# A two-layer transformer kernel: layernorms, expert work, shift rows and weight loads placed anew in its first attention layer

## The chip, the cores and the metric

The kernel runs on one core of a Trainium2 chip. The metric is the device time of one execution in microseconds; the kernel before takes 1212.92 us (median of three runs, 1212.03 to 1213.0). All arithmetic is float32, apart from a mask and a bias fold that go through TensorE in bfloat16 pieces.

## What is computed

Four sequences of 512 tokens with 256 features pass through four residual steps, each on a layernormed input:

```
x = x + attention_0(layernorm(x))   # 16 heads of 16, causal, over the 512 tokens of a sequence
x = x + experts_0(layernorm(x))     # for each output feature: router over 8 experts, the top 2 of the softmax
x = x + attention_1(layernorm(x))   # 16 query heads of 128, 4 key/value heads, over the batch of 4 at each position
x = x + mlp_1(layernorm(x))         # gated, 2048 wide, 4-bit weights with scales
```

In the experts a token gets 256 x 8 router logits, so each of the 256 output features picks its own two experts; the result is the weighted sum of those two experts' outputs. Router and experts have biases.

## The kernel before

**Tiling.** `xres` holds all 2048 tokens on chip, as 16 tiles of 128 tokens. Block j (0 to 3) is tiles 4j to 4j+3: tokens 128j to 128j+127 of all four sequences. Causal attention of block j needs the keys of blocks 0 to j.

**Attention 0.** `norm_pieces` normalises a block (statistics and scaling on VectorE, the inverse root on GpSimd, called POOL in the profile). `prepare` (L561) transposes the result on TensorE, `project` (L524) makes queries and keys, two heads' groups at a time, and sends them by 8 DMAs each into the tile `qk`, and `values` (L546) makes the values in `va`. In `qk` each head has 32 partitions: row 0 is a shift row, rows 1 to 16 hold the head's features. The shift row of the keys is 1 and that of the queries minus the row's greatest score, so that the second scores come out shifted. `blank` (L455) prepares `qk` and `va` of a later block with memsets on POOL.

The work is cut into 44 batches (L594): block 0 has 4 (one for each sequence, all 16 heads), block 1 has 8 (8 heads each), blocks 2 and 3 have 16 each (4 heads each). In batch n's turn of the loop at L776, the program emits `greatest(n+1)` (scores, L606), `shift(n)` (L639: the maxima of batch n are transposed, one 128x128 transpose for each group of four heads, and subtracted), `mask(n+1)` (L621: causal mask added by matmuls, then maxima by VectorE), a slot of filler, `mixed(n-1)` (L691: probabilities times values), `powers(n)` (L654: second scores, exponentials on ScalarE, a causal select on POOL), and a second slot of filler. `divided` (L712) finishes a sequence: transpose, division, transpose back, and after the last sequence of a block the output product and the residual.

**The planner.** TensorE, VectorE and POOL execute in program order here. What fills the slots comes from generators in the list `streams`: each yields `need(engine, cost, gap, cond)` ahead of a piece, and `fill` (L140) runs through the list from the front and takes pieces while the engine's budget for this slot is above zero, the gap in slots since that stream's last piece has passed, and the condition holds. Budgets for TensorE are 4.0 and 4.0 in block 0, 2.0 and 2.4 in block 1, and less after; VectorE gets 2.6. The streams are the next block's `prepare`, `divided`, `fold_pieces` (L234: biases added to the weights of router and experts by a matmul and two additions), `hidden_pieces` (L256: layernorm and transposes of a finished block for the experts), `logit_pieces` (router products), `weight_pieces` (top 2 and softmax weights on VectorE and ScalarE), `result_pieces` (expert products) and `addition_pieces`. Products of router and experts that are not done within attention 0 are spread over attention 1 by the counter `products_left` (L254, L1082).

**Shared things.** Small matmul results go to a pool `dn` of two PSUM buffers; scores to a pool of five. SP issues most DMAs: x, the projections' outputs, and the router and expert weights `rw` and `ew` (`load_pair`, L515), 16 transfers of 256 KB, two after each of batches 0 to 7. The biases come as 96 rows (three copies) to `bs`, and POOL splits them into bfloat16 parts in `blanks` (L488).

**Start.** Three idle matmuls run when `w_project` has landed; then all of `prepare(0)`, `greatest(0)` and `mask(0)` precede the loop.

Of the kernel before, what the change touches and what calls it, by code (L numbers as in the profile page):

```python
# [32 lines left out]
def tile_transformer(  # L33
# [200 lines left out]
    def fold_pieces():  # L234
# [3 lines left out]
        for i, w in enumerate((rw, ew)):  # L238
            for c in range(4):
                yield need(  # L240
                    "DVE", 1.4, cond=lambda i=i, c=c: slot >= loaded.get((i, c), slot) + 3
# [189 lines left out]

    with ExitStack() as l0:
# [12 lines left out]
        shift_row = mask32[:, 0:1]  # L445


        qk = w0.tile([P, 4, NBLK + 2, NS, P], F32, name="qk")
        maxes = [w0.tile([P, 4, 4, 32], F32, name=f"mx{i}") for i in range(2)]
# [5 lines left out]
        def blank(j, i):  # L455

            keys = qk[:, :, j].rearrange("p g s q -> p g (s q)")
            if i == 4:
                to = va.shape[1] if j == NBLK - 1 else (j + 1) * per_block
                nc.gpsimd.memset(va[:, j * per_block : to], 1.0)  # L460
                nc.gpsimd.memset(keys[96:97], 1.0)
            elif i:
                nc.gpsimd.memset(keys[32 * i - 32 : 32 * i - 31], 1.0)
            else:
                nc.gpsimd.memset(keys, 0.0)
# [4 lines left out]
            shift_row.unsqueeze(1).to_broadcast([P, 4, 512]),  # L470
# [11 lines left out]
        bs = a3.tile([P, 2, 512], F32, tag="pt", name="bs")  # L482
        nc.sync.dma_start(out=bs[0:96], in_=bias)
# [4 lines left out]
        def blanks(xn):  # L488
# [6 lines left out]
            for i in range(5):  # L495
                blank(1, i)
# [3 lines left out]
            br = a3.tile([P, 512], F32, tag="pt", name="br")[0:96]  # L500
            bh = a1.tile([P, 512], BF16, tag="oq", name="bh")[0:96]
# [22 lines left out]
        def project(j, xT, half, stage, i):  # L524
# [9 lines left out]
            if i:  # L534
                to = 4 + j % 2
                for r in range(8):
# [3 lines left out]
                        out=qk[h + 1 : h + 17, 2 * half + r // 4, j : to + 1 : to - j].rearrange(  # L540
# [20 lines left out]
        def prepare(j):  # L561

            out = []
            yield from norm_pieces(j, b1, b2, out)
            if not j:
                blanks(out[0])
            xT = a1.tile([P, 2, NS, P], F32, tag="xT0", name=f"xT0_{j}")
            for hc in range(2):
                yield need("PE", 0.5, 1 - hc)
                ps = transposed(out[0], hc, ps_dn, "dn", f"x0_ps{j}_{hc}")  # L570
                nc.scalar.copy(
# [5 lines left out]
            normed.clear()  # L577
            for half in range(2):
                if j or half:
                    stage = a1.tile([P, 2, 512], F32, tag="stage", name=f"stage{j}_{half}")  # L580
                else:
                    stage = b2.tile([P, NE, HID], F32, tag="lg", name="stage0")
                    stage = stage.rearrange("p e o -> p (e o)")[:, :1024].rearrange(
                        "p (i q) -> p i q", i=2
                    )
                for i in range(2):
                    yield need("PE", 1.75, 0 if half or i else 1)
                    project(j, xT, half, stage, i)
                if half == (not j):
                    for s in (0, 2):  # L590
                        yield need("PE", 1.75)
                        values(j, xT, s)

# [27 lines left out]
        def mask(n):  # L621
# [4 lines left out]
            for ps in tiles:  # L626
                for b in range(nb):
                    to = b * nk + j * P
                    nc.tensor.matmul(  # L629
                        ps[:, to : to + P], lhsT=ident_h, rhs=later,  # L630
                        start=False, stop=b == nb - 1,
                    )
            for h, ps in enumerate(tiles):
                nc.vector.tensor_reduce(  # L634
                    maxes[n % 2][:, :nb, h, 0],
# [3 lines left out]
        def shift(n):  # L639
# [3 lines left out]
            ps = ps_mm.tile([P, 4, P], F32, tag="mm", name=f"mxT_{n}")  # L643
            for b in range(len(gs)):
                nc.tensor.transpose(  # L645
                    ps[:, b], maxes[n % 2][:, b].rearrange("p h d -> p (h d)"), ident
                )
            g, nb = gs[0], len(gs)
            q = qk[:, g : g + nb, 4 + j % 2, s, :]
            nc.vector.tensor_tensor(q, q, ps[:, :nb], ALU.subtract)  # L650
# [61 lines left out]
        def divided(j, s):  # L712
# [27 lines left out]
            for t in (0, 2):  # L740
                yield need("PE", 1.75, 1)
# [10 lines left out]
                yield need("DVE", 0.7, 1)  # L752
# [3 lines left out]
            streams.insert(fold_at, Stream(hidden_pieces(j)))  # L756
# [9 lines left out]
        for piece in prepare(0):  # L766
            pass
        nc.sync.dma_start(out=wo, in_=w_out.rearrange("(k p) o -> p k o", p=P))
        greatest(0)
        mask(0)  # L770
        fold = Stream(fold_pieces())
        streams += [
            fold, Stream(addition_pieces()), Stream(counted(weight_pieces())), Stream(result_pieces()),
            Stream(logit_pieces()),
        ]
        for n in range(NBT):  # L776
            j, s, gs = batches[n]
            if (not n or batches[n - 1][0] != j) and j + 1 < NBLK:
                inputs = Stream(prepare(j + 1))
                streams.insert(0, inputs)  # L780
            if n + 1 < NBT and batches[n + 1][0] != j:
                while inputs.next is not None:
# [8 lines left out]
            fill(PE=(4.0, 2.0, 1.8, 1.6)[j], DVE=2.6)  # L791
            with tc.high_priority(offset=AHEAD):
                if n:
                    mixed(n - 1)
                powers(n)
            if n and batches[n - 1][2][-1] == 3:
                streams.insert(0, Stream(divided(*batches[n - 1][:2])))
            fill(PE=(4.0, 2.4, 2.2, 2.0)[j], DVE=2.6)
            if n < 8:
                w, dram = (rw, router_w) if n < 4 else (ew, expert_w)  # L800
                load_pair(w, dram, 2 * n % 8)
                load_pair(w, dram, 2 * n % 8 + 1)
                loaded[n // 4, n % 4] = slot
            if 1 <= n < 11:
                blank(2 + (n - 1) // 5, (n - 1) % 5)
            if n in (2, 6):
                load_x(n // 4 + 2)
# [447 lines left out]
```

## Time and profile before

| | |
|---|---|
| median of the runs | 1212.92 us |
| profiled execution | 1213.42 us |
| its span in the profile | 1211.7 us |
| mean granted TensorE clock | 0.989 |
| attention 0, experts beside it | to about 420 us |
| attention 1, rest of the experts beside it | about 420 to 880 us |
| MLP | about 880 us to the end |

The profile is of one execution on the chip. Engines are PE (TensorE's matmuls), PEld (its weight loads, which overlap matmuls), DVE (VectorE), ACT (ScalarE), POOL (GpSimd) and SP (which only issues DMAs; SPq and ACTq lines are issues). A group or a line in order of time gives the source line, the engine, the operation, output and inputs by their tile names, and the count; in brackets stands idle time of that engine just before, and what ended it. A float32 matmul counts as two instructions. The clock is the share of full TensorE speed that was granted.

### The profile page before, as it was taken

The numbers are of one execution on the slowest core, as the hardware profiler recorded it, in microseconds if no ns is written. First come the engines' busy times: TensorE is split into PE (matmuls) and PEld (weight loads), VectorE is DVE, ScalarE is ACT, GpSimd is POOL, SyncE is SP. The second block draws the span as 40 slices with busy tenths as digits, with TensorE's granted clock in tenths as the row PEclk, the third lists the DMA queues.
The fourth block names the chain that finished last, engine by engine and source line by source line (L and its number), as shares of the span: only waits on it lengthen the run. The fifth ranks groups of instructions, "written<-read, shape, count | busy, mean of one in ns | idle before, by whom it ended". The sixth has DMA issues, their size and how long they took to land.

```text
span 1211.7 us, 18780 instructions
## 1 busy us (share of the span) xinstructions
PE 1168.9 (96%) x7278; PEld 679.8 (56%) x7278; DVE 802.6 (66%) x1780; ACT 485.5 (40%) x1101; POOL 121.1 (10%) x155
## 2 busy tenths in 40 slices
PE   6979999999999898999999999999999999999998
PEld 3656555555555543555555555656645456475487
DVE  2555589898887848737886395798499853735710
ACT  1233455664555444434444345355344321312300
POOL 8333321121111000000000000000000000000000
PEclk9899999999999998999999999999999999999999
DMA  7122102000000040000000001021020000000000
GB/s 221 17 56 54 19 4 34 2 1 1 2 1 2 27 147 1 1 1 1 1 1 1 1 1 36 10 55 43 1 62 9 1 1 17 1 1 18 0 1 35
DMA packets 21305, 26.78 MB, mean 22 GB/s; under 512 B 5120, under 2 KB 14592, under 8 KB 21216
## 3 DMA queue, kind: packets, MB, share of 16 engines
q1 hardware_dynamic: 20544, 24.40, 7.6%
q10 hardware_dynamic: 672, 1.18, 0.4%
q8 instruction: 57, 0.93, 0.3%
q14 instruction: 32, 0.26, 0.1%
HBM read 19.27 MB, written 2.10 MB: 18 GB/s over the span
## 4 chain that ended last, share of the span: by engine, by line
PE 81%; DVE 12%; ACT 2%; DMA 2%; issue 1%; SPq 1%; POOL 0%; ACTq 0%; DVEq 0%; POOLq 0%
PE qk_ps L928 10%; PE o L1019 9%; PE y L1175 9%; PE g L856 8%; PE u L856 8%; PE eo L226 8%; PE lg_ps L226 7%; PE s L614 4%; DVE mx L634 3%; PE s L664 3%; PE av L700 2%; PE v_ps L910 2%; PE qk_ps L529 2%; PE s L941 1%; PE a L999 1%
## 5 line engine op out<-in xcount | busy, mean ns | idle before, releaser
L928 PE MATMUL qk_ps<-xT,wqkv 128*128 128x512 f32 x320 | 148.7, 599 | 0.6 <-ACT qT L932 0.6
L226 PE MATMUL lg_ps<-rw,xT 128*128 128x512 f32 x256 | 123.8, 607 | 3.7 <-ACT xT L895 1.7
L226 PE MATMUL eo<-ew,xT 128*128 128x512 f32 x256 | 122.0, 600 | 1.3 <-ACT part L315 1.0
L1019 PE MATMUL o<-wpj,oT 128*128 128x256 f32 x512 | 119.8, 382 | 0.0
L634 DVE TENSOR_REDUCE mx<-s 128x1 f32<-128x384 f32 (+3 forms) x176 | 100.5, 634 | 20.3 <-PE s L629 20.3
L1175 PE MATMUL y<-wd,it 128*128 128x256 f32 x512 | 111.8, 379 | 0.0
L1019 PEld LDWEIGHTS o<-wpj,oT 128*128 128x128 f32 x512 | 95.9, 190 | 28.1 <-issue 15.1
L1175 PEld LDWEIGHTS y<-wd,it 128*128 128x128 f32 x512 | 97.1, 190 | 14.9 <-issue 2.2
L928 PEld LDWEIGHTS qk_ps<-xT,wqkv 128*128 128x128 f32 x320 | 59.3, 190 | 70.0 <-issue 60.2
L673 ACT ACTIVATE pt<-s 128x512 f32<-128x512 f32 (+1 forms) x176 | 83.7, 561 | 34.4 <-PE s L664 34.3
L856 PE MATMUL g<-xT,wgu 128*128 128x512 f32 x192 | 90.4, 593 | 0.0
L856 PE MATMUL u<-xT,wgu 128*128 128x512 f32 x192 | 90.2, 592 | 0.0
L315 ACT ACTIVATE part<-eo,c 128x256 f32<-128x256 f32 x128 | 53.7, 473 | 81.5 <-PE eo L226 76.9
L683 POOL TENSOR_SCALAR_AFFINE_SELECT pt<-pt 128x256 f32<-128x256 f32 (+2 forms) x88 | 55.2, 632 | 268.6 <-ACT pt L673 268.1
L1153 ACT ACTIVATE th<-sq 128x512 f32<-128x512 f32 x64 | 40.3, 629 | 87.6 <-DVE sq L1152 87.6
L177 POOL TENSOR_TENSOR ln_rs<-rs_v,minus_half 128x4 f32<-128x4 f32 x16 | 18.0, 1127 | 563.3 <-DVE rs_v L176 457.9
L226 PEld LDWEIGHTS lg_ps<-rw,xT 128*128 128x128 f32 x256 | 46.5, 192 | 49.0 <-issue 36.9
L226 PEld LDWEIGHTS eo<-ew,xT 128*128 128x128 f32 x256 | 46.4, 190 | 45.8 <-issue 37.0
L614 PE MATMUL s<-qk 32*128 32x128 f32 (+3 forms) x512 | 69.7, 478 | 1.3 <-DMA qk<-stage 0.5
L214 DVE TENSOR_TENSOR xres<-xres,y 128x256 f32<-128x256 f32 x16 | 6.7, 421 | 92.2 <-PE y L1175 92.2
L650 DVE TENSOR_TENSOR qk<-qk,mxT 128x128 f32<-128x128 f32 (+2 forms) x44 | 15.2, 346 | 77.0 <-PE mxT L645 69.3
L289 ACT COPY lg<-lg_ps 128x512 f32<-128x512 f32 x64 | 37.6, 587 | 64.5 <-PE lg_ps L226 64.3
(233 smaller groups left out, 1831.2 us busy)
## 6 DMA issues: line engine op xcount, KB each, us to landing
qk<-stage SPq DMA_DIRECT2D x56, 64.0 KB, 2.4
wqkv<-in_w_qkv SPq DMA_DIRECT2D x8, 320.0 KB, 6.0
rw<-in_router_w SPq DMA_DIRECT2D x8, 256.0 KB, 4.8
ew<-in_expert_w SPq DMA_DIRECT2D x8, 256.0 KB, 5.0
wpj<-in_w_proj SPq DMA_DIRECT2D x1, 2048.0 KB, 11.9
out<-xres SPq DMA_DIRECT2D x4, 512.0 KB, 2.6
xres<-in_x SPq DMA_DIRECT2D x3, 512.0 KB, 8.1
dq_wgu<-in_gate_w SPq DMA_DIRECT2D x8, 128.0 KB, 2.4
```

The costliest lines, as they stand in the source:

```text
L226: nc.tensor.matmul(ps, lhsT=xT[:, hc, (g % 4) * P : (g % 4 + 1) * P], rhs=w[:, hc, 2 * pair : 2 * pair + 2, :].rearrange("p e o -> p (e o) ...
L289: nc.scalar.copy(lg[:, 2 * pair : 2 * pair + 2, :].rearrange("p e o -> p (e o)"), ps)
L315: nc.scalar.mul(part[:, e % 4], ps[:, i], c[:, e : e + 1])
L614: nc.tensor.matmul(tiles[h][:, b * nk : (b + 1) * nk].rearrange("p (c k) -> p c k", k=P), lhsT=queries(j, g)[r, s], rhs=qk[r, g, : j + 1, ...
L634: nc.vector.tensor_reduce(maxes[n % 2][:, :nb, h, 0], ps[:, : nb * nk].rearrange("p (b k) -> p b k", b=nb), AX.X, ALU.max,)
L673: nc.scalar.activation(pt[:, i, : nb * nk], tiles[2 * pair + i][:, : nb * nk], AF.Exp, scale=0.25)
L683: nc.gpsimd.affine_select(out=last, in_=last, compare_op=ALU.is_ge, fill=0.0, base=0, pattern=pattern, channel_multiplier=-1,)
L856: nc.tensor.matmul(ps, lhsT=wgu[:, w, half, jj, par * P : (par + 1) * P], rhs=xT[:, half, :], start=half == 0, stop=half == 1,)
L928: nc.tensor.matmul(ps, lhsT=wqkv[:, hc, kv, h, :], rhs=xT[:, hc, :], start=hc == 0, stop=hc == 1,)
L1019: nc.tensor.matmul(ys[t // 2][:, t % 2], lhsT=state["o"][:, h, t * P : (t + 1) * P], rhs=wpj[:, HPK * kv + h, :], start=kv == 0 and h == 0 ...
L1153: nc.scalar.activation(th, sq, AF.Tanh, scale=0.7978845608028654)
L1175: nc.tensor.matmul(ps, lhsT=it[:, c // 2, c % 2, t * P : (t + 1) * P], rhs=wd[:, c // 2, c % 2, :], start=c == 0, stop=c == 2 * NJ - 1,)
```

## The change

- **Four shift rows to a head.** Each head has rows 0 to 3 for shifts and its features in rows 4 to 19. Keys of group i have a 1 in row i alone. All maxima of a batch lie in one 128x128 tile, so `shift` makes one transpose, whose result is subtracted from all groups of the batch; `mask` makes one matmul for each score tile, with the mask repeated along the columns. `blank` writes one group's keys of a block with one copy (512 columns) in place of a memset of all groups and four one-row memsets.
- **Blocks 1 to 3 normalised ahead.** Block 1 is normalised before the loop, right after block 0, and its transposes follow block 0's projections (copied out of PSUM by VectorE); its projections are a stream from the start. `prepare(2)` enters at batch 1 and `prepare(3)` at batch 7, in place of batches 4 and 12; for them values come before queries and keys, and queries and keys wait until the batches that read the old queries are done.
- **Block 0's tokens for the experts at once.** Its two output products come in one slot, and `hidden_pieces(0)` goes to the front of the list.
- **Pieces evenly by slot.** TensorE's budgets in block 0 are 2.0 and 2.4 in place of 4.0 and 4.0; folds come one to a slot.
- **Loads.** Router and expert weights are loaded four transfers after each of batches 0 to 3; x of blocks 2 and 3 after batches 0 and 2 (before: 2 and 6). The biases are loaded three times as 8 rows into a tile cleared by VectorE, and are split on POOL after block 1's blanking.

```diff
-                    "DVE", 1.4, cond=lambda i=i, c=c: slot >= loaded.get((i, c), slot) + 3
+                    "DVE", 1.4, 1, cond=lambda i=i, c=c: slot >= loaded.get((i, c), slot) + 3
...
-        maxes = [w0.tile([P, 4, 4, 32], F32, name=f"mx{i}") for i in range(2)]
+        maxes = [w0.tile([P, 4, 32], F32, name=f"mx{i}") for i in range(2)]
...
             if i == 4:
                 to = va.shape[1] if j == NBLK - 1 else (j + 1) * per_block
                 nc.gpsimd.memset(va[:, j * per_block : to], 1.0)
-                nc.gpsimd.memset(keys[96:97], 1.0)
-            elif i:
-                nc.gpsimd.memset(keys[32 * i - 32 : 32 * i - 31], 1.0)
             else:
-                nc.gpsimd.memset(keys, 0.0)
+                nc.gpsimd.tensor_copy(
+                    qk[:, i, j].rearrange("p s q -> p (s q)"),
+                    mask32[:, i : i + 1].to_broadcast([P, 512]),
+                )
...
-        bs = a3.tile([P, 2, 512], F32, tag="pt", name="bs")
-        nc.sync.dma_start(out=bs[0:96], in_=bias)
+        bs = b1.tile([P, 2, 512], F32, tag="hi4", name="bs")
+        nc.vector.memset(bs, 0.0)
+        for i in range(3):
+            nc.sync.dma_start(out=bs[32 * i : 32 * i + 8], in_=bias)
...
-                        out=qk[h + 1 : h + 17, 2 * half + r // 4, j : to + 1 : to - j].rearrange(
+                        out=qk[h + 4 : h + 20, 2 * half + r // 4, j : to + 1 : to - j].rearrange(
...
+        def projections(j, xT):
+            if j > 1:
+                for s in (0, 2):
+                    yield need("PE", 1.75, 1, cond=lambda: blanked > 5 * j - 10)
+                    values(j, xT, s)
             for half in range(2):
...
+                for i in range(2):
+                    yield need(
+                        "PE", 1.75, 0 if half or i else 1,
+                        cond=lambda: j < 2 or done >= 8 * j - 12 and blanked >= 5 * j - 5,
                     )
                     project(j, xT, half, stage, i)
...
             for ps in tiles:
-                for b in range(nb):
-                    to = b * nk + j * P
-                    nc.tensor.matmul(
-                        ps[:, to : to + P], lhsT=ident_h, rhs=later,
-                        start=False, stop=b == nb - 1,
-                    )
+                nc.tensor.matmul(
+                    ps[:, : nb * nk].rearrange("p (b k) -> p b k", b=nb)[:, :, j * P :],
+                    lhsT=ident_h, rhs=later.unsqueeze(1).to_broadcast([P, nb, P]),
+                    start=False, stop=True,
+                )
...
-            ps = ps_mm.tile([P, 4, P], F32, tag="mm", name=f"mxT_{n}")
-            for b in range(len(gs)):
-                nc.tensor.transpose(
-                    ps[:, b], maxes[n % 2][:, b].rearrange("p h d -> p (h d)"), ident
-                )
+            ps = ps_mm.tile([P, P], F32, tag="mm", name=f"mxT_{n}")
+            nc.tensor.transpose(ps, maxes[n % 2].rearrange("p h g -> p (h g)"), ident)
             g, nb = gs[0], len(gs)
             q = qk[:, g : g + nb, 4 + j % 2, s, :]
-            nc.vector.tensor_tensor(q, q, ps[:, :nb], ALU.subtract)
+            nc.vector.tensor_tensor(
+                q, q, ps.unsqueeze(1).to_broadcast([P, nb, P]), ALU.subtract
+            )
...
-                yield need("PE", 1.75, 1)
+                yield need("PE", 1.75, 1 if j or not t else 0)
...
-                yield need("DVE", 0.7, 1)
+                if j:
+                    yield need("DVE", 0.7, 1)
...
-            streams.insert(fold_at, Stream(hidden_pieces(j)))
+            streams.insert(fold_at if j else 0, Stream(hidden_pieces(j)))
...
-        for piece in prepare(0):
+        nc.sync.dma_start(out=wo, in_=w_out.rearrange("(k p) o -> p k o", p=P))
+        both = [[], []]
+        for j in range(2):
+            for piece in norm_pieces(j, b1, b2, both[j]):
+                pass
+            normed.clear()
+            if not j:
+                blanks(both[0][0])
+                xT = a1.tile([P, 2, NS, P], F32, tag="xT0", name="xT0_0")
+                for piece in inputs_T(0, both[0][0], xT):
+                    pass
+        for i in range(5):
+            blank(1, i)
+        split_biases()
+        for piece in projections(0, xT):
             pass
-        nc.sync.dma_start(out=wo, in_=w_out.rearrange("(k p) o -> p k o", p=P))
+        xT = unused("xT0_1", "p (h s q) -> p h s q", h=2, s=NS)
+        for piece in inputs_T(1, both[1][0], xT):
+            pass
         greatest(0)
         mask(0)
+        inputs = {1: Stream(projections(1, xT))}
+        done = blanked = 0
...
-            if (not n or batches[n - 1][0] != j) and j + 1 < NBLK:
-                inputs = Stream(prepare(j + 1))
-                streams.insert(0, inputs)
+            if n in (1, 7):
+                to = 2 if n == 1 else 3
+                inputs[to] = Stream(prepare(to))
+                streams.insert(0, inputs[to])
...
-            fill(PE=(4.0, 2.0, 1.8, 1.6)[j], DVE=2.6)
+            fill(PE=(2.0, 2.0, 1.8, 1.6)[j], DVE=2.6)
...
-            fill(PE=(4.0, 2.4, 2.2, 2.0)[j], DVE=2.6)
-            if n < 8:
-                w, dram = (rw, router_w) if n < 4 else (ew, expert_w)
-                load_pair(w, dram, 2 * n % 8)
-                load_pair(w, dram, 2 * n % 8 + 1)
-                loaded[n // 4, n % 4] = slot
-            if 1 <= n < 11:
-                blank(2 + (n - 1) // 5, (n - 1) % 5)
-            if n in (2, 6):
-                load_x(n // 4 + 2)
+            fill(PE=(2.4, 2.4, 2.2, 2.0)[j], DVE=2.6)
+            if n < 4:
+                w, dram = (rw, router_w) if n < 2 else (ew, expert_w)
+                for i in range(4):
+                    load_pair(w, dram, 4 * n % 8 + i)
+                    loaded[n // 2, (4 * n % 8 + i) // 2] = slot
+            for _ in range(1 + (n < 2) if blanked < 10 else 0):
+                blank(2 + blanked // 5, (blanked + 4) % 5)
+                blanked += 1
+            if n in (0, 2):
+                load_x(n // 2 + 2)
```

## The prediction

> **What bounds the kernel now.** I read the page's first part, then busy time in stretches of the span, then TensorE's instructions in order of time, then the groups, then the queue that issues transfers.
>
> ```profile
> span 1211.7 us, 18780 instructions
> PE 1168.9 (96%) x7278; PEld 679.8 (56%) x7278; DVE 802.6 (66%) x1780; ACT 485.5 (40%) x1101; POOL 121.1 (10%) x155
> ```
>
> TensorE (PE) is the bound: 1168.9 of 1211.7 us, so a change can win only by filling its 42.8 idle microseconds, by keeping its clock up, or by taking matmuls away. Where the idle time lies (columns: stretch, its length, then busy time and instructions of each engine, the granted clock):
>
> ```profile
> 0.00:30.00 30.00, 20.32 (x80) 11.24 (x81) 7.46 (x21) 5.67 (x9) 25.10 (x30) 1.00 0.73 223
> 30.00:120.00 90.00, 77.70 (x924) 55.44 (x923) 50.29 (x102) 29.16 (x58) 31.48 (x36) 0.91 0.19 43
> 120.00:200.00 80.00, 75.03 (x853) 45.30 (x845) 59.38 (x143) 38.38 (x94) 23.85 (x29) 1.00 0.11 18
> 200.00:410.00 210.00, 207.17 (x2113) 111.17 (x2112) 179.22 (x439) 117.01 (x320) 31.32 (x54) 0.99 0.01 3
> 520.00:1180.00 660.00, 658.43 (x2774) 380.42 (x2774) 429.89 (x878) 246.77 (x496) 7.00 (x6) 1.00 0.05 12
> ```
>
> From 200 us on there is next to nothing to gain, and a microsecond saved earlier arrives at the end: the expert products are a stock (products_left) that is spread over what follows. The change works at 0 to 200 us: 9.7 idle in the start, 12.3 in 30 to 120 (at a mean clock of 0.91), 5.0 in 120 to 200. What a stall looks like there:
>
> ```profile
> 81.57 0.66 PE L718 MATMUL av_T<-ident,avs 128*128 128x128 f32 x4
> 84.03 0.44 PE L733 MATMUL oq_T<-ident,oq 128*128 128x128 f32 x2 [1.81 <-DVE oq L725]
> ...
> 87.08 1.06 PE L629 MATMUL s<-later,ident_h 128*128 128x128 bf16 x8
> 89.46 1.08 PE L202 MATMUL x_ps<-ident,xn 128*128 128x128 f32 x4 [1.31 <-DVE rw L250]
> 91.22 1.12 PE L202 MATMUL x_ps<-ident,xn 128*128 128x128 f32 x4 [0.68 <-ACT xT L571]
> 93.01 0.58 PE L244 MATMUL fold<-rows 128*128 128x512 bf16 x1 [0.67 <-ACT xT L571]
> ```
>
> Small transposes wait for VectorE (DVE), which has a layernorm, a fold and the softmax division queued in one slot, while no large product is there to fill in. The mask matmuls at 87.08 take 1.06 us where the same eight take 0.61 at 102.66: the clock has dropped.
>
> **What the Trainium skill says.** "TensorE: Matmul & The Clock Gate", Part 1 (The HAM clock gate): after about 3.4 us of idling the array runs at half clock until it has been busy as long. The trace agrees in kind: mean clock 0.66 in 30 to 40 us, 0.80 and 0.69 in 80 to 100; it drops there with gaps of 1 to 2 us, though, so scattered gaps do it too. "DMA: Bandwidth & Descriptors", Issuing engines are not separate DMA queues: transfers of both queues share 16 engines; agreed, their busy share is 0.81 in each of the first two 10 us, and the 64 KB key transfers then land after 3.5 us where they take 2.4 alone. "GPSIMD Engine Reference", 4.1 Engine selection: a one-input operation runs about at line rate there; the POOL rows below show cost by elements per partition, not partitions.
>
> **The change, part by part.** Times of one execution, 1213.42 us; its span is 1211.7, with 1.7 around it. The median of the runs shown is 0.5 lower.
>
> (1) *Four shift rows: one transpose of the maxima to a batch.* Groups:
>
> ```profile
> L645 PE MATMUL mxT<-ident,mx 128*128 128x128 f32 x64 | 17.3, 324 | 0.0
> L629 PE MATMUL s<-later,ident_h 128*128 128x128 bf16 x256 | 22.8, 228 | 0.0
> L463 POOL MEMSET qk<- 1x2048 f32 x9 | 16.2, 1800 | 0.4
> ```
>
> Starts in order of time give what they occupy: four transposes 0.50 us (54.62 to 55.12), two 0.28, one 0.16. Four batches of block 0 save 0.34 each, eight of block 1 save 0.11 (rounded down): 2.2 us off PE, on the path. VectorE's subtraction keeps its 512, 256 or 128 columns: 0. The mask goes from 256 matmuls to 176 but streams as many columns; sixteen narrow ones occupy 0.89 us, four of 512 columns about 4 x 0.22 (the fold product of this width): 0, at best 0.1 in twelve batches, 1 us. A repeated operand isn't in the trace; nothing suggests it streams slower.
>
> (2) *Blanking* falls on POOL from 5 x 1.80 + 1.01 = 10.0 us a block to four copies of 512 columns (a quarter of the 1.89 us copy, 0.5 to 0.7 with overhead) + 1.01, so about 3.3. POOL is 10% busy: 0 on the path. It eases the SBUF access shared with VectorE (xn takes 2.93 us at 42.09, 1.38 at 8.74), uncounted.
>
> (3) *Start.* Added to VectorE before its first layernorm: a memset of 1024 columns, 0.9 us (the 1088-column one takes 0.96). It hides: xn ends at 10.1, the first transpose starts at 13.4 behind the idle matmuls. Without that cover it costs 0.9. Block 1's layernorm (4 x 0.58 + 0.17 + 1.0 on POOL + 1.38 = 4.9) and two copies out of PSUM (0.7 each, by the 0.68 us addition at L754) go into VectorE's 20.3 idle microseconds before 30.4. Its eight transposes (1.2 us) go on PE between the values, which end at 26.5, and the first scores, whose last input lands at 29.48: hidden, 0.3 late at most. Queued behind these on PE are all scores; behind the copies on VectorE, the first maxima. On SP, the three bias transfers (96 KB for 384) wait for the memset; block 1's x is queued after them in program order, and could be issued at about 7 in place of 2.2 and land at 15 in place of 10.3: still before 26.5. Taken as 0.
>
> (4) *Block 0 and 1, evenly.* Spacing of the twelve batches is given by the transposes of the maxima: 34.4, 41.8, 54.6, 70.1, 77.7, 86.6, 102.4, 110.7, 120.3 for batches 0 to 8. I walked the new planner by its own budgets (2.0 and 2.4 for each pair of slots). Batch 0 gets two projections and one value pair (3 x 1.72 = 5.2 us) where it had no PE filler; batch 1 value, projection; batch 2 block 2's transposes, a projection, values; batches 3 to 5 block 2's rest. Folds, one to a slot, take slots 5 to 12. Both output products (2 x 1.72) go in slot 13, and block 0's layernorm starts there; first router products in slot 15, batch 7, against batch 9 now (132.54). With each batch at the larger of its PE sum (4.3 us of attention in block 0, 3.9 in block 1, plus filler) and DVE sum, and 1.5 us for a product that waits for the second buffer of the dn pool, batch 8 comes at 109 in place of 120.3, with about 9 us more of PE work done (two projections, two router products, transposes). Of that 20 us, 2.2 is (1). But the same arithmetic on batches 4 and 5 of before gives about 16 us where they took 24.7: waits on three engines add up as the sums do not show. So I count the pools themselves: 16.0 us of PE idle at 30 to 170 (12.3, and 3.7 of the next 50), and 2.9 us lost to the second clock dip (1.06 for 0.61, 1.94 for 1.08, and so on). I take half the idle, 8.0, and the dip, 2.9. The first dip, at 30.9 to 37, stays: the same wait for keys precedes it. New gaps are likely in slots 11, 12 and 14, where nothing large is ready; they are in the half not taken.
>
> (5) *Loads in four steps, x earlier.* Same bytes, same issue time of about 0.5 us each; no VectorE wait for these weights shows now. The fold keeps three slots' grace, but slots differ in length. 0.6 for a late x of block 2 (needed in batch 1); bounds 0 and the slower rival below.
>
> Sum: 2.2 + 8.0 + 2.9 - 0.6 = 12.5. 1213.4 - 12.5 = 1200.9, less 0.5: **1200.5**.
>
> **Rivals.** (a) *Nearly all idle goes*: 14 + 2.9 + 2.2 + 1 = 20, so 1193. For it: my batch walk. Against: VectorE is as long as PE in batches 5 and 6, and the pool of two dn buffers is unchanged. 14%. (b) *The waits only move*: layernorms of blocks 2 and 0 still sit in front of the maxima on VectorE, so idle time shrinks by 2 us and the clock dips elsewhere; 2.2 + 2 remain: 1208.5. 17%. (c) *Slower, by SP's order*: weight loads and key transfers share SP, which issues in order.
>
> ```profile
> 69.76 5.04 SPq L539 DMA_DIRECT2D qk<-stage  x8
> 74.85 1.06 SPq L518 DMA_DIRECT2D rw<-in_router_w  x2
> ```
>
> Eight key transfers hold it 5 us, and wait for ScalarE's copy first. If the last expert weights are queued behind block 2's keys (slot 9, about 77 us), they land at 77 + 5 + 1 + 5 = 88, and the fold due at 77 holds VectorE, and all maxima behind it, for 11; a second such hold at slot 11, 6. 17 - 12.5 = 4.5 over before: 1217.5. It decides from 12.5 us of fold waits. Against: half the weights are issued before 13 us now, and in program order every load precedes block 2's keys. 11%. (d) Within 0.2%: an even mix of these, 4%.
>
> **How the numbers follow.** Main case 54%, its own range 1196 to 1206. Faster by over 0.2% (2.4 us, about what a measurement of this kernel can tell from no change): 54 + 14 + 17 = 85%; same 4%; slower 11%. The range 1192 to 1209 takes in (a) and (b), and leaves out (c), (d) and the tails, about 20%.
>
> **What would show it.** Right: maxima transposes x44; PE idle in 30 to 120 at about 6 us and no dip near 80 to 100; first router product before 115; batch 8 at 109 to 115. Wrong: PE idle or a low clock moved to batches 5 to 9; a VectorE wait for rw or ew; the first scores later than 31 us; or idle time after 410 us that grew.

## The result, and the profile after

| | before | after |
|---|---|---|
| median | 1212.1 us (1212.0 to 1213.0, 5 runs) | 1228.7 us (1224.5 to 1230.0, 5 runs) |
| ratio | | 1.0127, 95% interval 1.0109 to 1.0145 |
| profiled execution, its span | 1213.4, 1211.7 us | 1226.1, 1224.3 us |
| TensorE idle in the span | 42.8 us | 54.1 us |

The change makes the kernel 1.3% slower. The forecast was 1200.5 us, with 1192 to 1209 as its range. The page of the kernel after, its first part:

```profile
span 1224.3 us, 18602 instructions
PE 1170.2 (96%) x7178; PEld 672.7 (55%) x7178; DVE 805.4 (66%) x1783; ACT 483.7 (40%) x1099; POOL 101.4 (8%) x152
```

A hundred TensorE instructions are gone and POOL has 20 us less to do, as reckoned, but TensorE's busy time rose by 1.3 us and its idle time by 11.3. Busy time in stretches, the same columns as before:

```profile
0.00:30.00 30.00, 21.46 (x96) 12.17 (x96) 15.94 (x40) 5.68 (x9) 23.25 (x40) 1.00 0.72 214
30.00:120.00 90.00, 75.69 (x833) 47.81 (x832) 50.72 (x105) 30.64 (x60) 20.92 (x26) 0.96 0.22 48
120.00:200.00 80.00, 73.41 (x756) 42.88 (x755) 48.76 (x110) 33.83 (x85) 11.49 (x20) 0.95 0.08 15
200.00:410.00 210.00, 202.57 (x2022) 108.72 (x2024) 176.84 (x426) 112.33 (x308) 33.98 (x54) 0.97 0.01 2
520.00:1180.00 660.00, 657.46 (x2778) 375.20 (x2777) 430.14 (x878) 249.16 (x504) 6.09 (x6) 1.00 0.05 12
```

Idle time did not fall in 30 to 120 us (12.3 before, 14.3 now), and it grew where the forecast saw nothing to gain or lose: 2.8 to 7.4 us in 200 to 410. Between 120 and 200 us VectorE was busy 59.4 us before and is busy 48.8 now.

The transposes of the maxima are milestones that both kernels pass in the same order. From their starts (the time of batch 3, then what passes between milestones, us):

```
                  batch 3    3-5    5-8   8-14  14-27  27-43  43-end    span
before               70.1   16.5   33.7   50.1   95.9  134.2  811.2  1211.7
after                63.6   28.5   29.2   59.0   96.0  137.1  810.8  1224.3
```

The kernel after is 6.5 us ahead at batch 3, loses 12.0 by batch 5, regains 4.5, loses 8.9 from batch 8 to 14, and 2.9 from 27 to 43. It has more TensorE work behind it meanwhile. Filler products can be counted by the records; one of four instructions takes 1.72 us at full clock (0.43 from each start to the next). At batch 14 the kernel after has done six more than the kernel before (block 3's four projections and two value products, 10.3 us), at batch 27 one more, at batch 43 two more. So it comes to batch 14 10.0 us later with 10.3 us more done: it is level with the kernel before, and its lead of the first batches is gone. The stretch from 14 to 27 then has five products (8.6 us) fewer and takes 96.0 us for 95.9: TensorE is idle 4.0 us there for 1.6, at a clock of 0.96 for 1.00.

**Batches 3 to 5.** Four engines of the kernel after in order of time, first SP's issues of block 2's keys, then ScalarE's copies, TensorE and VectorE:

```profile
80.64 19.86 SPq L539 DMA_DIRECT2D qk<-stage  x14
```

```profile
79.98 0.59 ACT L533 COPY stage<-qk_ps 128x512 f32<-128x512 f32 x1 [3.95 <-PE qk_ps L529]
...
88.97 0.59 ACT L533 COPY stage<-qk_ps 128x512 f32<-128x512 f32 x1 [3.46 <-DMA qk<-stage]
```

```profile
85.57 1.98 PE L529 MATMUL qk_ps<-xT,wp 128*128 128x512 f32 x4 [1.65 <-ACT aT L751]
89.61 0.58 PE L244 MATMUL fold<-rows 128*128 128x512 bf16 x1 [2.06 <-ACT stage L533]
90.12 2.09 PE L631 MATMUL s<-qk 32*128 32x256 f32 x16
```

```profile
76.49 1.28 DVE L250 TENSOR_TENSOR rw<-rw,fold 128x512 f32<-128x512 f32 x2 [7.62 <-PE fold L244]
...
90.23 1.28 DVE L250 TENSOR_TENSOR ew<-ew,fold 128x512 f32<-128x512 f32 x2 [7.78 <-PE fold L244]
```

The staging tile (`stage`, from which the DMAs take the projections' outputs) has one buffer. With the values first, the two halves of the projections follow each other, so the copy of half 1 waits for the eight transfers of half 0 (issued from 80.64 us). It holds a `dn` buffer meanwhile; the fold product behind it on TensorE waits 2.06 us, then sixteen score products take 2.09 us, for 1.15 in the batch before: half the clock. VectorE, next in line for the fold, has stood for 7.78 us, with this batch's maxima behind it.

**Batches 8 to 14.** VectorE's lines at the boundary of the experts' tiles 0 and 1, before and then after (L420 ends a tile's weights, L363 begins the next tile's):

```profile
190.19 0.20 DVE L420 SCALAR_TENSOR_TENSOR c<-sums,c 128x8 f32<-128x8 f32 x1
190.31 1.21 DVE L363 TENSOR_TENSOR hi<-lg 128x1024 f32<-128x1024 f32 x1
```

```profile
171.77 0.17 DVE L420 SCALAR_TENSOR_TENSOR c<-sums,c 128x8 f32<-128x8 f32 x1
...
180.75 0.29 DVE L663 TENSOR_TENSOR qk<-qk,mxT 128x128 f32<-128x128 f32 x1 [8.81 <-PE mxT L660]
...
191.25 1.21 DVE L363 TENSOR_TENSOR hi<-lg 128x1024 f32<-128x1024 f32 x1
```

Tile 0 is done 18.4 us earlier than before, and tile 1 starts 0.9 us later: the chain of the experts' weights stands still for 19.5 us. What TensorE does there instead:

```profile
165.86 1.88 PE L529 MATMUL qk_ps<-xT,wp 128*128 128x512 f32 x4
...
171.81 3.50 PE L529 MATMUL qk_ps<-xT,wp 128*128 128x512 f32 x4 [2.73 <-DVE sums L419]
...
177.62 1.98 PE L226 MATMUL eo<-ew,xT 128*128 128x512 f32 x4
...
182.56 1.88 PE L226 MATMUL eo<-ew,xT 128*128 128x512 f32 x4
...
186.04 1.98 PE L226 MATMUL lg_ps<-rw,xT 128*128 128x512 f32 x4
```

Block 3's four held projections (two of them, at 156.93 and 161.61, not shown) are first in the planner's list once batch 11 is past, then come expert and output products. They take the place of tile 1's last router product (186.04), on which VectorE depends. The view of VectorE's waits in 120 to 200 us, before and after (columns: who waits for whom, us in total, times, longest):

```profile
DVE qk L650 <- PE mxT L645: 15.6, 6, 6.5
```

```profile
DVE qk L663 <- PE mxT L660: 31.4, 7, 9.1
```

VectorE, without weight work to do, stands at the next batch's transpose for 15.8 us more.

### The profile page after: what moved, and what is told of

Same layout as the page of the kernel before. It is cut to its first block, busy times and chain, and to the rows that moved or that the text cites. A ratio compares the mean times of both kernels' runs of the same rounds, so it can differ in the third digit from the quotient of the medians.

```text
span 1224.3 us, 18602 instructions
## 1 busy us (share of the span) xinstructions
PE 1170.2 (96%) x7178; PEld 672.7 (55%) x7178; DVE 805.4 (66%) x1783; ACT 483.7 (40%) x1099; POOL 101.4 (8%) x152
## 3 DMA queue, kind: packets, MB, share of 16 engines
q10 hardware_dynamic: 672, 1.18, 0.4%
## 4 chain that ended last, share of the span: by engine, by line
PE 80%; DVE 13%; ACT 3%; issue 1%; DMA 1%; POOL 1%; SPq 1%; ACTq 0%; DVEq 0%; POOLq 0%
PE qk_ps L965 10%; PE y L1212 9%; PE o L1056 9%; PE g L893 8%; PE u L893 8%; PE lg_ps L226 8%; PE eo L226 7%; PE s L631 5%; DVE mx L650 3%; PE s L679 2%; PE v_ps L947 2%; PE av L715 2%; PE qk_ps L529 2%; PE a L1036 1%; PE s L978 1%
## 5 line engine op out<-in xcount | busy, mean ns | idle before, releaser
L226 PE MATMUL lg_ps<-rw,xT 128*128 128x512 f32 x256 | 129.1, 628 | 6.9 <-ACT part L315 2.9
L226 PEld LDWEIGHTS eo<-ew,xT 128*128 128x128 f32 x256 | 46.2, 190 | 48.8 <-issue 36.8
L342 DVE TENSOR_TENSOR part<-part 128x512 f32<-128x512 f32 x32 | 22.1, 691 | 67.1 <-ACT part L315 67.1
```

Source lines behind the costliest of these rows:

```text
L226: nc.tensor.matmul(ps, lhsT=xT[:, hc, (g % 4) * P : (g % 4 + 1) * P], rhs=w[:, hc, 2 * pair : 2 * pair + 2, :].rearrange("p e o -> p (e o) ...
```

## The experiments

Ratios are to the kernel before, with 95% intervals. The first milestone differs by up to 4 us between runs of the same start (batch 3 at 62.6 to 66.5 us), so it is the later stretches that are compared. The stretches of a kernel come from one profiled execution, which need not lie at its median. Theory 1 when the experiments began: the standstill of the expert chain is the loss. Theory 2: the staging waits are.

**The four shift rows alone**, put into the kernel before (the diff's edits of `blank`, `project`, `mask` and `shift`, and nothing else).

> The kernel before with the four shift rows alone: one transpose for each batch, one mask matmul for each score tile, POOL's copies in place of memsets. By the prediction's part 1 it saves 2.2 us (20 transposes): 1209 to 1211. Rival: a repeated operand streams slower, or freed TensorE time in block 0 only becomes waiting, 1212 or more.

1215.1 us, 1.0020 (1.0009 to 1.0032): a miss. Its stretch from 30 to 120 us:

```profile
30.00:120.00 90.00, 79.51 (x841) 53.92 (x842) 48.51 (x102) 29.41 (x58) 20.04 (x25) 0.83 0.18 42
```

The clock there fell from 0.91 to 0.83: TensorE has fewer instructions there (841 for 924 by the records) and was busy 1.8 us longer, since more of them ran at half speed. The profiled execution (1217.6 us) is one of the slower of 20, but the whole set shows the same: its mean clock over the span is 0.980 in the median (0.976 to 0.987), against 0.987 (0.979 to 0.989) in 40 runs of the kernel before.

**Block 3 later**: batch 12, where the kernel before began it.

```diff
-            if n in (1, 7):
+            if n in (1, 12):
```

> The changed kernel, but block 3 is prepared from batch 12 on, as before, and not from batch 7. Theory 1 (the experts starve: the four projections of block 3, held back until batch 12 and then first in the list, take TensorE's budget from the last router product of token tile 1, so VectorE's weight work stands still for 19.5 us between tile 0 and tile 1): that gap falls below 3 us and about 10 us of the 16 come back, 1217 to 1220. Theory 2 (what is lost is lost by waits for the one stage buffer and the two dn buffers in batches 3 to 5, and the clock dips behind them): only the 2.7 us wait of a block 3 projection at 169 us and the dip behind it go, 1224 to 1227.

1213.2 us, 1.0002 (0.9987 to 1.0016). The gap after tile 0 closes to 0.1 us; 15.5 us come back, more than theory 1's 10, with batches 3 to 5 as slow as ever (27.7 us).

**Values between the halves**, as before the change, for blocks 2 and 3.

```diff
             for half in range(2):
                 ...
-                if half == (not j) and j < 2:
+                if half == (not j):
```

> The changed kernel, but blocks 2 and 3 make their values between the two halves of queries and keys, as before, so that the stage buffer has two slots more to be sent. Theory 2: the waits of 2.1 and 2.7 us for it go, and the half clock behind each, together about 7 us, 1221 to 1223. Theory 1: six pieces of block 3 in place of four now stand before the router products from batch 12 on, the gap grows, 1228 to 1233.

1212.2 us, 0.9998 (0.9984 to 1.0012). That looks like theory 2 at twice its size, but the gap after tile 0, which theory 1 saw growing, closed here too (164.22 to 164.30 us): block 3's values no longer took slots ahead of the router products. The run couldn't tell the two apart, so later runs split it by block.

**Block 3's projections wait for the router products**, the program otherwise unchanged.

```diff
-                        cond=lambda: j < 2 or done >= 8 * j - 12 and blanked >= 5 * j - 5,
+                        cond=lambda: j < 2 or done >= 8 * j - 12 and blanked >= 5 * j - 5
+                        and (j < 3 or len(logits) + len(weights) > 1),
```

> The changed kernel, but block 3's projections also wait until tile 1 has its router products (one more condition). Theory 1: the gap in VectorE's weight work closes, 1217 to 1221. Theory 2: nothing but order changes, the waits for buffers stay, 1226 to 1230.

1206.2 us, 0.9943 (0.9919 to 0.9966): 22.6 us come back, more than the loss. Its VectorE at the same place:

```profile
171.78 0.17 DVE L420 SCALAR_TENSOR_TENSOR c<-sums,c 128x8 f32<-128x8 f32 x1
171.87 1.22 DVE L363 TENSOR_TENSOR hi<-lg 128x1024 f32<-128x1024 f32 x1
```

**Values between, block 2 alone and block 3 alone** (`j in (2,)` or `j in (3,)` added to the condition above, and the same block taken out of `if j > 1`).

> The changed kernel with block 2's values put back between its two halves of projections; block 3's stay first. Theory 1 (VectorE's chain over the experts' tiles stands still for 19.5 us, from 171.8 to 191.3 us, because block 3's projections take the places of the router products): batches 3 to 5 lose the waits for the staging buffer and come some 6 us earlier, but the gap between tile 0 done and tile 1 started stays over 12 us and the end gains at most 2 to 8 us: 1221 to 1227. Theory 2 (the staging buffer's waits explain the loss): nearly all comes back, 1212 to 1214.

1216.4 us, 1.0030 (1.0020 to 1.0041). The whole gains 12.3 us, over theory 1's 2 to 8 and short of theory 2. Batches 3 to 5 take 22.2 us in place of 28.5, as forecast; the gap shrank too, to 5.6 us, because the other order moved the pieces behind it.

> The changed kernel with block 3's values put back between its two halves; block 2's stay first. Theory 1: block 3's values then wait behind the held projections, the router products of tile 1 take their places before batch 12, the gap in VectorE's expert work closes to under 3 us while batches 3 to 5 stay as slow as in the changed kernel (13 to 15 us each): 1213 to 1218. Theory 2: only block 3's own wait of 2.7 us and the one copy after it go, at most 4.3 us: 1224.

1206.7 us, 0.9954 (0.9938 to 0.9971): 22.0 us back, more than either theory allowed, with batches 3 to 5 nearly as slow as in the kernel after (27.2 us). Theory 2 is not the main cause.

**Both mends** (projections wait, block 2's values between).

> The changed kernel with both mends: block 3's projections wait until router products and weights are more than one tile ahead, and block 2's values lie between its halves. If the two causes are separate and add up: 1206.2 less 4 to 8, so 1198 to 1202. If the staging waits of batches 3 to 5 are absorbed later once the expert chain runs without a gap: 1205 to 1207.

1211.9 us, 0.9988 (0.9979 to 0.9997). The mends don't add up. Milestones:

```
                  batch 3    3-5    5-8   8-14  14-27  27-43  43-end    span
router first         63.3   27.6   30.5   57.7   99.0  124.0   801.8  1203.9
between, block 3     63.7   27.2   28.8   55.7  101.5  125.7   801.8  1204.3
both                 63.7   21.7   31.4   51.8   96.0  135.4   809.2  1209.2
```

*Router first* and *between, block 3* gain little where the mend is made. Against the kernel after they gain 11 to 13 us from batch 27 to 43 and 9 after it, for 3 to 5 lost from 14 to 27. In *both*, batch 27 comes 12 to 14 us earlier than in these two, and the far gain is absent.

A part of it is work done at another time. From batch 27 to 43 *both* and the kernel after make 14 router and 14 expert products by the records, *router first* and *between, block 3* 13 of each, having made the others earlier: 3.4 us at 1.72 each. After batch 43 all four have the same 32 and 40 products left; there TensorE is idle 11.4 us in *router first* for 17.2 in the kernel after.

**The standstill alone, in the kernel before**: tile 1's last router product is held back.

```diff
                     g // 4 in xTs and (0, pair) in folded and (g < 2 or g - 2 in weights) and made() >= at
+                    and ((g, pair) != (1, 3) or slot >= 38),
```

> The kernel before with one thing changed: the last router product of tile 1 is held back by the planner until slot 38, so that VectorE's work on tile 1 starts some 19 to 21 us after tile 0 is done, and nothing else of the change is there. Theory 1 (the expert chain is paced by VectorE and a standstill in it arrives at the end): 13 to 19 us slower than before, 1225 to 1232. Rival (TensorE is the bound, the chain has slack and catches up): at most 3 us slower, 1212 to 1215.

1223.7 us, 1.0105 (1.0073 to 1.0138), so 11.4 us slower: under theory 1's 13 to 19, far over the rival's 3. VectorE's boundary here:

```profile
192.16 0.20 DVE L421 SCALAR_TENSOR_TENSOR c<-sums,c 128x8 f32<-128x8 f32 x1
...
213.79 1.21 DVE L364 TENSOR_TENSOR hi<-lg 128x1024 f32<-128x1024 f32 x1
```

The profiled execution is the slowest of four (1231.4 us at a mean clock of 0.976; the others 1222.7 to 1224.5 at 0.987), so its stretches show 18 us and not 11.4. In it the standstill of 21.4 us costs 6.8 us from batch 14 to 27 and gives 4.0 back by 43; 14.2 come after batch 43 (825.4 for 811.2). Most of that is work put off: three router and three expert products (10.3 us), which the kernel before has done by batch 43, are still to do.

**Is VectorE the pace, or TensorE?** VectorE's subtraction at L389 left out for tiles 0 to 6, then TensorE's product doubled.

```diff
+                if g > 6:
                     tt(d[:, e : e + 4], d[:, e : e + 4], ..., ALU.subtract)
```

> The changed kernel without the subtraction of the second largest router value from the router's results of tiles 0 to 6 (two VectorE instructions of 1.2 us each to a tile, 16.5 us in all; the order of everything else is the same, and the experts' weights of these tiles are other numbers). Theory 1 (from batch 14 on VectorE sets the pace of attention 0, TensorE only fills): from batch 14 to batch 43, 233.1 us in the changed kernel, falls by 8 to 16, and the whole to 1212 to 1221. Rival (TensorE sets the pace there): at most 2 us, 1226 to 1229.

1222.4 us, 1.0091 (1.0065 to 1.0116), 6.4 us less than the kernel after. From batch 14 to 43 VectorE is busy 14.2 us less (181.0 for 195.2), and the stretch gains 2.9 us; the one after it is the same (810.7). VectorE alone isn't the pace.

```diff
+                for _ in range(2 if h < 7 and not pair else 1):
                     dense(ps.rearrange("p e o -> p (e o)"), h, ew, pair)
```

> The changed kernel with the first of the four output products of the experts done twice for tiles 0 to 6 (2 matmuls of 0.86 us each more to a tile, 12.0 us of TensorE in all; the second overwrites the first, the order of everything else is the same). Theory 1 (VectorE sets the pace from batch 14 to 43): TensorE's 7.4 idle us and part of its half-clock time between 200 and 410 us take up most of it: 0 to 5 us slower, 1228 to 1234. Rival (TensorE sets the pace): all 12 us arrive, 1239 to 1242.

1233.6 us, 1.0173 (1.0158 to 1.0188): 4.9 of 12 us arrive. That is within theory 1's 0 to 5, but not for its reason. The page:

```profile
span 1231.0 us, 18659 instructions
PE 1176.0 (96%) x7206; PEld 675.2 (55%) x7206; DVE 805.3 (65%) x1783; ACT 483.6 (39%) x1099; POOL 99.7 (8%) x152
```

TensorE's idle time took up nothing (55.0 us for 54.1). Its busy time rose by 5.8 us for 12 us of work, because the granted clock rose: 0.991 to 0.992 over the span in all four runs, for 0.984 to 0.989 in the kernel after. By the means (0.005 of 1229 us) that is some 6 us, an estimate. So all of the added work shows, less what the clock gave back, and whether TensorE is the pace stays open.

**Is it the order after the last batch?**

```diff
         while last.next is not None:
-            fill(PE=2.0, DVE=2.6)
+            fill(PE=2.4, DVE=2.6)
```

> The changed kernel with one budget of the planner altered: in the slots after the last batch of attention 0, TensorE is given 2.4 in place of 2.0, so that one more router product comes ahead of attention 1's first products; everything up to batch 43 has the same order. From the last transpose of the maxima to the end the changed kernel took 810.8 us, and the two runs in which that order was different took 801.8. Theory 3 (the order at the start of attention 1 alone decides these 9 us): that stretch falls to 800 to 805 and the whole to 1217 to 1221. Rival (the 9 us came from the expert chain being further ahead when attention 0 ends): under 2 us, 1226 to 1229.

1221.9 us, 1.0077 (1.0050 to 1.0104). The last stretch gave 3.1 us (807.7), not 6 to 11: the order there is part of the 9 us and not all. The median gained 6.9 us, the profiled execution 0.9.

**Block 3 from batch 9**, with both mends and then alone (`if n in (1, 9)`).

> Both mends of the changed kernel (block 3's projections wait for router products, block 2's values lie between its halves) and block 3's own preparation taken up from batch 9 in place of 7. By its program the order at the start of attention 1 is then that of the two runs that took 801.8 us from the last transpose of the maxima. If the gains up to batch 43 (399.95 us) and that stretch are independent: 1201 to 1204. If one is bought with the other: 1206 or more, as before.

1199.1 us, 0.9888 (0.9871 to 0.9906): the fastest, 13 us under the kernel before.

> The changed kernel with block 3's preparation taken up from batch 9 in place of 7, one number. Theory 4: by its program it has the order at the start of attention 1 that took 801.8 us, and its router products of tile 1 come before block 3's projections: 1204 to 1210, with batches 3 to 5 as slow as in the changed kernel. Rival (the preparation's start matters only together with the other two mends): 1216 or more.

1211.7 us (1203.0 to 1216.2 over 16 runs), 0.9976 (0.9958 to 0.9995). Its median is 17 us below the kernel after for one number, short of the 1204 to 1210 expected. Its profiled execution is the second fastest of the sixteen (1204.5 us, span 1202.7), so its stretches flatter it:

```
                  batch 3    3-5    5-8   8-14  14-27  27-43  43-end    span
block 3 from 9       63.5   27.1   28.8   54.0  100.3  125.7   803.4  1202.7
both and from 9      63.5   22.2   31.9   52.6  100.0  124.0   803.0  1197.2
```

The far gains, 11 to 13 us from batch 27 to 43 and 7 to 8 after it, come with the batch, with or without the other mends. Block 2's order gains 4.9 us in batches 3 to 5, of which 3.1 are lost again by batch 8. VectorE's wait for the transposes in 120 to 200 us is, in the fastest version:

```profile
DVE qk L664 <- PE mxT L661: 17.7, 7, 5.3
```

**Does an order with the chain further on do it?** The planner is told 0.05 for the subtractions of 1.25, with the work kept and then left out.

```diff
-                yield need("DVE", 1.25)
+                yield need("DVE", 1.25 if g > 6 else 0.05)
```

> The changed kernel with a lie in the planner's table: the two subtractions of the second largest router value are put down at 0.05 in place of 1.25 each for tiles 0 to 6, while they are still done. The work is the same; only the written order changes, with the expert chain further on in any given batch. Theory 4 (the written order decides: how far the chain has come by the batches of block 3): 1214 to 1220, with the stretch from batch 14 to 43 under 228 us and the last one at 801 to 803. Rival (an order that overfills VectorE's slots makes it wait more): 1228 or more.

1225.5 us, 1.0098 (1.0074 to 1.0123): a miss. The last stretch falls to 805.0, but batches 14 to 43 take 236.1 us for 233.1.

> The changed kernel without those two subtractions in tiles 0 to 6 (16.5 us of VectorE left out, so that the experts' weights are other numbers), and with the planner told so. Theory 4: the same work left out gave 3 to 6 us where the planner did not know of it; with the order written for it 1206 to 1214. Rival (the order matters little): 1220 to 1223, as without being told.

1218.8 us, 1.0046 (1.0026 to 1.0067). Told of it, the planner makes 10 us of the 16.5 left out, where 6 came untold; 1206 to 1214 was expected.

**The four rows taken back in the fastest version.**

> The fastest version so far (1199.1: both mends, block 3 from batch 9) with the four shift rows alone taken back to one shift row for each half. If the TensorE time that they free arrives where waits are few: 2 to 3 us slower, 1201 to 1202. If it goes into waits as it did in the kernel before: within 1.5 us.

1204.0 us, 0.9923 (0.9899 to 0.9948), against 0.9888 (0.9871 to 0.9906): 4.9 us by the medians where 2 to 3 or under 1.5 were expected, 2.8 by the profiled spans, and intervals that overlap by a little. Here the rows gain; what they gain is not sharp. Nor need it be TensorE's transposes: the profiled executions differ by 3.0 us at batch 3 already (66.5 for 63.5), where VectorE has been busy 42.5 us for 34.3. With the one row back, POOL's memsets run beside VectorE's layernorms again (last section).

## Why the prediction was wrong

**Step (4), the idle time of 30 to 170 us: wrong in sign.** It held 10.9 of the 12.5 us forecast. Half of 16.0 us of idle was to go, with batch 8 at 109 to 115 us and first router products before 115. The router product came at 114.16, as forecast; batch 8 came at 121.35, and idle time rose by 2.0 us in 30 to 120 and by 11.3 in all. The walk through the budgets reckoned batches 3 to 5 as sums of costs; they held a wait that no cost shows. With the values first nothing stands between the halves, and a staging tile with one buffer puts SP's eight issues and a transfer between them. Values between the halves of block 2 gave back 6.3 us of the 12.0 lost there, and 12.3 us of the whole. Most of the other 5.7 is work done earlier: three projections and a value product (6.9 us) fall into this stretch, where the kernel before has none.

**The premise failed: "a microsecond saved earlier arrives at the end".** This is the larger error. It took TensorE's stock of products for the only thing that must be done in time. There is a second one, the chain router product, VectorE's weights, expert product, whose end attention 1 needs. `prepare(3)` at batch 7, ahead of everything in the list, held it for 19.5 us. That was visible in the diff (`streams.insert(0, ...)` and a condition that frees four projections at once), and I walked the planner only to batch 8. The change lost 16.6 us. Three ways of moving block 3's preparation off the router products (a later batch, in two settings; a condition; its values later) win back 15 to 23, and a standstill of like length alone costs the kernel before 11.4. That the preparation's place is the main cause is shown. That it costs by the standstill is not: with the gap closed, *router first* passes batch 14 only 1.4 us earlier (179.0 us for 180.4), and its gain comes after batch 27. In another order such a lead does arrive: the fastest version passes batch 14 level with the kernel before (170.2 us for 170.4), with five products (8.6 us) more done, and its span ends 14.5 us shorter.

**How the loss reaches the end is only partly shown.** VectorE as the pace from batch 14 on fell (16.5 us less gave 2.9 there); TensorE as the pace is not settled (4.9 of 12, beside a higher clock); that only the order after the last batch matters fell (3.1 of 9); that an order with the chain further on suffices fell too (236.1 us from batch 14 to 43 for 233.1). What stays: *router first*, *between, block 3* and the two versions with block 3 from batch 9 pass batch 27 at 270 to 278 us and take 124 to 126 us from there to batch 43; *both* and the run with values between pass it at 263 to 265 and take 135 to 137, like the kernel after (276, 137). Batch 27's time doesn't decide it: *between* for block 2 alone passes it at 271 and takes 136. One router and one expert product more (3.4 us) are a part of the difference; which pieces of the written order make the rest is open.

**The clock.** The forecast counted the second dip (2.9 us) as gone. The mean clock of 30 to 120 us did rise, 0.91 to 0.96, but 120 to 200 fell from 1.00 to 0.95 and 200 to 410 from 0.99 to 0.97: the dips moved. Over the span the clock is 0.987 for 0.989, some 2.6 us (an estimate, the lost shares times the spans), so it is a small part of the loss. Of the fastest version's 14.5 us of span it is more: at 0.994, some 6 us.

**Step (1)** was right in the count (44 transposes, 176 mask products) and wrong in "on the path": alone, its 2.2 us were not gained but 2.4 lost, and to the clock: TensorE's idle time fell to 40.8 us from 42.8, its busy time rose to 1175.1 from 1168.9. **Step (2)** held for POOL's time; its 0 on the path was not tested alone. **Step (3)** was set at 0 and has a part in the one gain that the kernel after shows: the first batches' transposes come 3.1 us earlier at batch 0 and 6.5 at batch 3, together with the evened slots, from which no run separates it. **Step (5)** was right on the loads: the last weights are issued at 60.61 us, ahead of block 2's keys.

**Rival (c)** had the side and one symptom, VectorE standing for folds: 24.2 us in 30 to 120 for 5.0 before. But its releaser was TensorE's fold product behind the staging wait, not a late weight load, so its mechanism did not occur. **Rival (b)**, that the waits only move, describes what came better than the main case, but it let idle time shrink by 2 us and the kernel gain (its sum gives 1208.7, not 1208.5). One of the forecast's own signs of being wrong is there: idle time after 410 us grew, from 13 to 17 us.

## What to carry to other kernels

When a planner's pieces are moved, follow not the sum of an engine's budget but each chain that crosses engines: ask which piece the inserted ones overtake, who is fed by it, and when that chain must end. When pieces move together, look at the single buffer that their old spacing hid. And since pieces placed anew change every later slot, test the neighbours of a setting: the batch at which block 3 begins was worth 13 to 17 us.

## What the runs showed of the hardware

**The granted clock moved when TensorE's work was changed.** With the four shift rows alone (20 transposes fewer, among other edits) the clock of 30 to 120 us was 0.83 for 0.91, and over the span 0.980 for 0.987 by the medians of 20 and 40 runs. With 12 us of products added it was 0.992 for 0.987. It isn't a rule: in the fastest version it was 0.994 with the four rows and 0.996 with one, by the profiled executions. Runs of one kernel differ by it too: the sixteen of block 3 from batch 9 go from 1203.0 us at 0.995 to 1216.2 at 0.986.

**Half clock after short waits.** "TensorE: Matmul & The Clock Gate" of the Trainium skill, Part 1 (The HAM clock gate), gives an idle window of about 3.4 us ahead of half clock. In the kernel after, products run at half speed behind a wait of 2.06 us (89.61 above), with one of 1.65 us four us earlier (85.57); no wait of TensorE from 60 to 90 us is longer than 2.06. So shorter waits were enough here; whether it took both is not shown.

**VectorE beside POOL.** A layernorm's scaling of 256 columns (`xn`) takes VectorE 0.37 to 0.42 us with POOL idle, 946 times in the 18 traces. It takes 1.17 to 1.18 us in 36 cases throughout beside POOL's causal select of 1024 columns, and 1.97 us in seven beside its memset of one partition and 2048 columns, which the change took out (one of them at 85.83 us in the kernel before).
